# Two half-filled experts in one slot: packing the rests of a mixture-of-experts layer

## The chip, the core and the metric

The kernel runs on one core of a Trainium2 chip. A core has a matrix engine (TensorE, PE in the profile; its weight loads are a row of their own, PEld), a vector engine (VectorE, DVE), a scalar engine (ScalarE, ACT), a general engine (GpSimd, POOL), a queue engine (SyncE, SP) and 16 DMA engines. The metric is the device time of one execution in microseconds (us), the median of several runs.

## The reference

Two layers work on `x` of 3327 rows by 256, with one 0/1 adjacency matrix of 3327 by 3327. Each layer is a graph part and a mixture-of-experts part, both added to `x`. The graph part of layer 0 and its experts, cut to what matters:

```python
x = x + _L0_gnn_ref(_layernorm(x), adj, W, b)     # mean over neighbours, times W
h = _layernorm(x)
probs = softmax(h @ gate_w + gate_b)              # 16 experts
top_probs, top_idx = top_k(probs, 2)              # each row goes to two experts
# for a row of expert e: y = (silu(h @ w1[e]) * (h @ w2[e])) @ w3[e], width 512 inside
x = x + sum over its two experts of  y * (top_prob / sum of both)
```

Layer 1 does the same with an attention-weighted graph part and 6 experts of three 256 by 256 matrices, also top 2 of 6.

## The kernel before

The work is in four stages, one after another with overlaps at the seams: graph of layer 0, slots of layer 0, graph of layer 1, slots of layer 1.

**Graph stages.** The function `graph` goes over column blocks of the transposed adjacency matrix. DVE turns each piece into a mask (L670), PE multiplies (L784), and a chain of small steps (`finish`, `dispatch`) follows each block: normalize, gate products (L810), softmax and top 2 on DVE, and a write of each row's number and weight into the list of its expert in DRAM (L371, indirect DMAs of POOL). Once all rows are routed, `slot_table` computes on DVE, from the counts per expert, which expert and which place in the list each slot has.

**Slots of layer 0.** A slot is 128 rows of one expert. `slots0` is a loop in which the parts of several slots stand side by side. For slot s+1 SP reads the expert's number from the table into a register and loads the hidden weights w1 and w2 (`load0_hidden`), for slot s the output weights w3 (`load0_out`); a load is skipped if the buffer already holds that expert. There are two sets of weight buffers, `w0[s % 2]`, and the table alternates between an expert of the first eight and one of the last eight, so that an expert's slots all use one set. SP also reads the place in the list and fetches 128 entries (`places`, L552); POOL gathers the rows (L560); PE transposes them (L579), makes the two hidden products (L956: 8 products each of 128x128 weights against 128 columns), ACT and DVE form silu times the other (L960, L964), PE makes the output product (L972: 4 products of 128x256), DVE multiplies by the routing weight (L975), and POOL adds the rows into DRAM (`rows_added`, L586). An add waits for the one before it. All three weight loads, the register reads and the list fetches of a slot stand in the one queue of SP, in the order of the loop.

There are 61 such slots (`USUAL0`): the usual number of slots when each expert's rows are rounded up to 128. If the routing needs more, a branch runs up to six more. The first 9 slots (`EARLY0`) have a table of their own and start before the graph stage has ended. The last 8 (from `LATE0`) add into a second tensor, so that the first can be read back before they are done. In the loop also stand loads and masks for the next graph stage (`graph1_ahead`), and one piece per slot of a repacking of the weights of layer 1 (`packs`, on ACT's queue).

**Slots of layer 1** are alike, with 256 rows each (L1137, L1149, L1152, L1154). Near their end four tiles `z` of 1 MB are cleared by DVE (L1187) before the results are read into them.

**Order of the work.** The program states an order, and a scheduler at build time arranges each engine's instructions by estimated times[...]. `tc.issue_after(x)` keeps an instruction behind `x`.

Of the kernel before, what the change touches and what calls it, by code (L numbers as in the profile page):

```python
# [25 lines left out]
def kernel(  # L26
# [52 lines left out]
    SLOTS0 = (2 * N - E0) // P + E0  # L79
# [10 lines left out]
    USUAL0 = min(SLOTS0, int(2 * N / P + E0 / 2 + (E0 / 12) ** 0.5))  # L90
# [8 lines left out]
    assert 2 * EARLY0 < LATE0  # L99

# [73 lines left out]
    later.append(halves_later)  # L174

# [114 lines left out]
    def dispatch(blk, logits, E, rows_of, seen, second_softmax):  # L290
# [78 lines left out]
        for j in range(n):  # L369
            for i in range(2):  # L370
                few_under_way("list", nc.gpsimd.indirect_dma_start(  # L371
                    out=rows_of[2 * (t0 + j) + i],
                    out_offset=bass.IndirectOffsetOnAxis(ap=idx[:, i, j : j + 1], axis=0),
                    in_=where[:, t0 + j, i, :], in_offset=None, bounds_check=E * NP - 1, oob_is_err=False,
                ))

    def slot_table(E, seen, size, slot_p, first=None, taken=None, two=False, low=None, late=None, finals=False):
# [18 lines left out]
        nc.vector.tensor_scalar(nt, ps[:, :E], float(0 if first else size - 1), None, op0=OP.add)  # L396
# [95 lines left out]
        out = small("s_out", 5, I32)  # L492
# [11 lines left out]
        return (out, had) if first else out  # L504

# [48 lines left out]

    def rows_in(who, of):

        n = who.shape[1]
        xg = io.tile([P, n, D], F32, name="xg", bufs=5 if n == 1 else 3)
        for h in range(n):
            last["pool"] = nc.gpsimd.indirect_dma_start(  # L560
                out=xg[:, h, :], out_offset=None, in_=of,
                in_offset=bass.IndirectOffsetOnAxis(ap=who[:, h, 1:2], axis=0),
            )
            if n > 1:
                few_under_way("slot", last["pool"])
        return xg
# [17 lines left out]
    def rows_added(who, y, to):  # L584

        nc.gpsimd.indirect_dma_start(  # L586
            out=to, out_offset=bass.IndirectOffsetOnAxis(ap=who[:, 0, 0:1], axis=0),
            in_=y, in_offset=None, compute_op=OP.add,
        )
# [113 lines left out]
    AHEAD = 3  # L703

    def graph_pools(name, st):
        y = st.enter_context(tc.tile_pool(name=f"y{name}", bufs=1, side="right")).tile([P, NT, 2, D], F32R, name=f"y{name}")
        return y, *(st.enter_context(tc.tile_pool(name=f"{n}{name}", bufs=b, side="right"))
                    for n, b in (("adjs", AHEAD), ("big", AHEAD), ("tmp", 4)))

# [5 lines left out]
    def graph(name, prepare, value, op, wx, update, after, steps, routed, between=None, pools=None, ahead=(), ready=None):  # L715
        adj_ahead, masks_ahead = ahead or ({}, {})
        with ExitStack() as st:
            y, adjs, big, tmp = pools or graph_pools(name, st)
# [198 lines left out]
    early = {}  # L917

# [22 lines left out]

    def load0_hidden(s, which):
        for i, w in enumerate((ffn0_w1, ffn0_w2)):
            load(w0[s % 2][i], lambda e: w[e].rearrange("o (p k) h -> p (o k) h", k=KD), which)

    def load0_out(s, which):
        load(w0[s % 2][2], lambda e: ffn0_w3[e].rearrange("o (a p b) d -> p (o a) b d", p=P, b=2), which)

    def hidden0(s, xT):
        ps = []  # L950
        for w in w0[s % 2][:2]:
            q = bank(2 if s < EARLY0 or s % 2 else 1, [P, NC0, P])
            for c in range(NC0):
                for k in range(KD):
                    h0 = (c // 2) * 2 * P + c % 2
                    nc.tensor.matmul(q[:, c, :], w[:, k, h0 : h0 + 2 * P - 1 : 2], xT[:, k, :],  # L956
                                     start=(k == 0), stop=(k == KD - 1))
            ps.append(q)
        hid = io.tile([P, NC0, P], F32, name="hid", bufs=2)
        silu = nc.scalar.activation(hid, ps[0], AF.Silu)  # L960
        if s >= EARLY0 + 4 and packs:
            with tc.issue_after(silu.ins):
                nc.scalar.dma_start(*packs.pop(0))
        last["silu"], last["hid"] = silu, nc.vector.tensor_mul(hid, hid, ps[1])  # L964
        last["act"], last["dve"] = last["silu"], last["hid"]
        return hid

    def out0(s, who, hid):
        w3 = w0[s % 2][2]
        ps = bank(1 if s < EARLY0 else 0, [P, 512])  # L970
        for c in range(NC0):
            last["slot"] = nc.tensor.matmul(ps[:, :D], hid[:, c, :], w3[:, c // 2, c % 2, :],  # L972
                                            start=(c == 0), stop=(c == NC0 - 1))
        y = io.tile([P, D], F32, name="y", bufs=4)
        nc.vector.tensor_scalar(y, ps[:, :D], weight(who, 0), None, op0=OP.mult)  # L975
        rows_added(who, y, xd_of[0] if s < EARLY0 else xd if s < LATE0 else xe)
# [4 lines left out]
    table0 = slot_table(E0, seen0, P, slot_p, taken=early["had"], two=True, low=seen_head, late=LATE0 - EARLY0)  # L981

    def table0_of(s):
        return (early["table"], s) if s < EARLY0 else (table0, s - EARLY0)
# [3 lines left out]
    def slots0(first, end):  # L988
        for s in range(first - 4, end + 1):
            if not first and s >= 2 * EARLY0 and s % 5 == 0 and s // 5 - AHEAD_AT < 2 * AHEAD:  # L990
                graph1_ahead(s // 5 - AHEAD_AT)
            if not first and s == 2 * EARLY0:
                or_any(table0, early["bad"])
            if not first and s == end - 4:
                early["more"] = asked(*table0_of(end))
            if first <= s + 1 < end:
                which[s + 1] = expert(*table0_of(s + 1), E0)
                load0_hidden(s + 1, which[s + 1])
            if first <= s < end:
                load0_out(s, which.pop(s))  # L1000
            known = EARLY0 if s < EARLY0 - 3 else end
            for i in range(max(who, default=-1) + 1, min(s + 6, known)):
                who[i] = places(*table0_of(i), E0, lists[0], P)
# [9 lines left out]
            if first <= s - 1:  # L1013
                out0(s - 1, who[s - 1], hid.pop(s - 1))
            if not first:
                head1(s - LATE0)
# [3 lines left out]
    pools1 = graph_pools("1", graph1)  # L1020
    ahead1 = {}, {}
# [68 lines left out]
    stage.close()  # L1090

# [9 lines left out]
    def after1(blk, hT):  # L1101
        n = len(blk)
        rh = work.tile([P, BT * P], F32, name="rh")
        ps = ps_mm.tile([P, BT * P], F32, name="mm")
        for k in range(KD):
            nc.tensor.matmul(ps[:, : n * P], small["rw1"][:, k, :], hT[:, k, : n * P], start=(k == 0), stop=(k == KD - 1))  # L1106
        nc.scalar.activation(rh[:, : n * P], ps[:, : n * P], AF.Relu, bias=small["rb1"])
        yield
        logits = choose(n, [rh], [small["rw2"]], E1, small["rb2"])
        yield  # L1110
        yield from dispatch(blk, logits, E1, views[1], seen1, True)
        yield
# [31 lines left out]
    def out1(s, who, h2):  # L1144
# [7 lines left out]
        last["dve"] = nc.vector.tensor_tensor(y, ps, w1s[s % 3][:, None, WB:BB].to_broadcast([P, 2, D]), op=OP.add)  # L1152
# [15 lines left out]
    def slots1(first, end):  # L1168
        for s in range(first - 3, end + 1):
# [15 lines left out]
            if not first and 0 <= s - LATE1 + len(LOW) < len(LOW):  # L1185
                z = zs[s - LATE1 + len(LOW)] = tail.tile([P, BT, 2, D], F32, name="z")
                nc.vector.memset(z, 0.0)  # L1187
# [62 lines left out]
```

## Time and profile before

| | |
|---|---|
| timed runs | 1063.59, 1067.03, 1070.9 us; median 1067.03 |
| the profiled execution | 1096.1 us, of which its span (first to last instruction) 1093.9 us |
| granted PE clock, mean | 0.947 |
| PE busy | 971.7 us |
| graph stage of layer 0, with the early slots at its end | 0 to about 290 us |
| the other slots of layer 0 | about 290 to 600 us |
| graph stage of layer 1 | about 600 to 850 us |
| slots of layer 1 and the end | about 850 to 1094 us |

How to read the lines. On the page a row of an engine gives its busy time, share of the span and number of instructions. A row of a timeline gives start, duration, engine, line of the kernel, operation, output<-inputs, shape and, in brackets, how long the engine had been idle and what ended that. Rows of like instructions are merged (x16). The program's f32 products appear as two instructions each. A row of a stage table gives the stretch in us, its length, the busy time of PE, PEld, DVE, ACT and POOL with the number of instructions, the granted PE clock, the mean share of the DMA engines that was busy, and GB/s.

### The profile page before, as it was taken

Reading aid. Unit: us, or ns where it says so; the run is one execution under the profiler, and the core shown is the slowest. Engines: PE = TensorE matmul, PEld = TensorE weight load, DVE = VectorE, ACT = ScalarE, POOL = GpSimd, SP = SyncE. Lnnn points to the kernel's source line nnn. Section 1 sums busy time; section 2 is a strip of 40 time slices with the busy share of each in tenths; the row PEclk is TensorE's granted clock in tenths of the full one; section 3 lists DMA queues with packets and bytes.
Section 4 is the critical chain, followed back from the end, with each engine's and each line's share of the span. In section 5 each row is a group of like instructions: output and inputs, shape, how many; then the busy total and the mean of one; then the engine's idle time right before and its main releaser. Section 6 shows DMA issues by size and latency. Waiting matters only on the chain. (4 is left out here: it accounts for less than half of the span.)

```text
span 1093.9 us, 17590 instructions
## 1 busy us (share of the span) xinstructions
PE 971.7 (89%) x5404; PEld 838.1 (77%) x5404; DVE 475.9 (44%) x1817; ACT 263.2 (24%) x556; POOL 415.3 (38%) x404
## 2 busy tenths in 40 slices
PE   7999988889899999999999789998986886989871
PEld 5778866779899999999998678876774675877750
DVE  6657565446222222122125386856843461112153
ACT  2312111223111111111114052222222332433320
POOL 2130154155544443443452411014416545556531
PEclk9999999799999999999999889999987898999986
DMA  9986694948858586667678699678491245645695
GB/s 335 339 295 205 232 297 105 319 121 260 252 117 258 124 223 178 169 170 190 166 185 257 152 277 298 181 248 213 121 303 30 74 148 179 240 140 188 203 308 176
DMA packets 122634, 226.33 MB, mean 207 GB/s; under 512 B 32258, under 2 KB 74626, under 8 KB 122540
## 3 DMA queue, kind: packets, MB, share of 16 engines
q1 hardware_dynamic: 76350, 169.29, 47.7%
q0 software_dynamic: 23664, 34.23, 14.6%
q10 hardware_dynamic: 22526, 21.67, 6.3%
q8 instruction: 44, 0.72, 0.3%
q14 instruction: 50, 0.41, 0.1%
HBM read 249.79 MB, written 39.46 MB: 264 GB/s over the span
## 5 line engine op out<-in xcount | busy, mean ns | idle before, releaser
L784 PE MATMUL acc<-big,y 128*128 128x512 f32 (+2 forms) x1456 | 354.3, 398 | 31.3 <-DVE big L670 20.5
L784 PEld LDWEIGHTS acc<-big,y 128*128 128x128 f32 (+1 forms) x1456 | 270.1, 198 | 88.1 <-DVE big L670 10.0
L956 PE MATMUL acc<-xT,w 128*128 128x128 f32 x1952 | 245.1, 284 | 1.6 <-DMA w<-in_ffn_w 1.6
L956 PEld LDWEIGHTS acc<-xT,w 128*128 128x128 f32 x1952 | 238.9, 198 | 2.3 <-PE acc L956 1.0
L371 POOL DMA_INDIRECT list<-where,t_idx x104 | 109.2, 1050 | 179.2 <-DVE t_idx L368 77.4
L560 POOL DMA_INDIRECT xg<-hd,who x119 | 116.6, 980 | 127.8 <-PE acc L579 44.0
L670 DVE TENSOR_SCALAR big<-adj 128x1536 fp32r<-128x1536 int32 (+8 forms) x136 | 112.0, 827 | 108.4 <-DMA adj<-in_adj_t 68.0
L586 POOL DMA_INDIRECT xd<-y,who x53 | 83.6, 1577 | 150.7 <-DMA xd<-y,who 71.9
L964 DVE TENSOR_TENSOR hid<-hid,acc 128x512 f32<-128x512 f32 x61 | 41.9, 688 | 199.1 <-PE acc L956 183.7
L972 PE MATMUL acc<-w,hid 128*128 128x256 f32 x488 | 116.8, 383 | 3.0 <-DVE hid L964 2.7
L972 PEld LDWEIGHTS acc<-w,hid 128*128 128x128 f32 x488 | 88.6, 192 | 13.3 <-DVE hid L964 3.1
L1140 ACT ACTIVATE h<-acc,v 128x256 f32<-128x256 f32 x116 | 54.6, 474 | 123.8 <-PE acc L1137 99.1
L594 POOL DMA_INDIRECT zd<-y,who x58 | 58.5, 1008 | 52.0 <-DVE y L1154 23.5
L581 ACT COPY xT<-mm 128x256 f32<-128x256 f32 (+1 forms) x74 | 32.2, 436 | 188.2 <-PE mm L579 140.9
L1137 PE MATMUL acc<-xT,v 128*128 128x256 f32 x232 | 67.7, 416 | 10.8 <-DMA v<-w1d 4.6
L1137 PE MATMUL acc<-h,v 128*128 128x256 f32 x232 | 64.2, 395 | 11.9 <-ACT h L1140 8.5
L1152 DVE TENSOR_TENSOR y<-acc,v 128x512 f32<-128x512 f32 x29 | 20.1, 692 | 121.0 <-PE acc L1149 69.9
L1137 PEld LDWEIGHTS acc<-xT,v 128*128 128x128 f32 x232 | 46.4, 212 | 22.8 <-issue 6.7
L1137 PEld LDWEIGHTS acc<-h,v 128*128 128x128 f32 x232 | 44.0, 199 | 23.6 <-ACT h L1140 13.2
L1149 PE MATMUL acc<-v,h 128*128 128x256 f32 x232 | 58.9, 392 | 1.3 <-ACT h L1140 0.9
L960 ACT ACTIVATE hid<-acc 128x512 f32<-128x512 f32 x61 | 36.4, 597 | 86.7 <-PE acc L956 79.9
L286 ACT ACTIVATE ln_h<-xs,ln_nmr,ln_rstd 128x256 f32<-128x256 f32 x58 | 30.5, 591 | 92.1 <-DVE ln_nmr L283 57.5
(265 smaller groups left out, 879.2 us busy)
## 6 DMA issues: line engine op xcount, KB each, us to landing
w<-in_ffn_w SPq DMA_DIRECT2D x183, 512.0 KB
adj<-in_adj_t SPq DMA_DIRECT2D x66, 768.0 KB
v<-w1d SPq DMA_DIRECT2D x29, 898.0 KB
adj<-in_adj_t SPq DMA_DIRECT2D x50, 512.0 KB
hd<-ln_h ACTq DMA_DIRECT2D x12, 512.0 KB
z<-zd SPq DMA_DIRECT2D x6, 1024.0 KB
adj<-in_adj_t SPq DMA_DIRECT2D x8, 765.0 KB
w1d<-in_ffn_w ACTq DMA_DIRECT2D x18, 256.0 KB
```

The source lines that it names most:

```text
L371: few_under_way("list", nc.gpsimd.indirect_dma_start(out=rows_of[2 * (t0 + j) + i], out_offset=bass.IndirectOffsetOnAxis(ap=idx[:, i, j : ...
L560: last["pool"] = nc.gpsimd.indirect_dma_start(out=xg[:, h, :], out_offset=None, in_=of, in_offset=bass.IndirectOffsetOnAxis(ap=who[:, h, 1 ...
L586: nc.gpsimd.indirect_dma_start(out=to, out_offset=bass.IndirectOffsetOnAxis(ap=who[:, 0, 0:1], axis=0), in_=y, in_offset=None, compute_op= ...
L594: last["z"] = nc.gpsimd.indirect_dma_start(out=zviews[n * s + h], out_offset=bass.IndirectOffsetOnAxis(ap=who[:, h, 0:1], axis=0), in_=y[: ...
L670: last["mask"] = nc.vector.tensor_scalar(mask[:kr, :, :cols], a[:kr, :, :cols], value, None, op0=op)
L784: last["graph"] = nc.tensor.matmul(acc[c][k][:, :w], y[:kr, j, part, k * P : (k + 1) * P], mask[:kr, jj, i0 : i0 + w], start=(j == 0 and p ...
L956: nc.tensor.matmul(q[:, c, :], w[:, k, h0 : h0 + 2 * P - 1 : 2], xT[:, k, :], start=(k == 0), stop=(k == KD - 1))
L964: last["silu"], last["hid"] = silu, nc.vector.tensor_mul(hid, hid, ps[1])
L972: last["slot"] = nc.tensor.matmul(ps[:, :D], hid[:, c, :], w3[:, c // 2, c % 2, :], start=(c == 0), stop=(c == NC0 - 1))
L1137: ins = nc.tensor.matmul(ps[:, c, :], w[:, k, c : H1 : NC1], src[:, k, :], start=(k == 0), stop=(k == 1))
L1140: last["act"] = nc.scalar.activation(dst[:, c, :], ps[:, c, :], AF.Relu, bias=w1s[s % 3][:, BB + 2 * i + c : BB + 2 * i + c + 1])
L1149: nc.tensor.matmul(ps[:, h, :], h2[:, c, h * P : (h + 1) * P], w[:, c, :], start=(c == 0), stop=(c == NC1 - 1))
```

## The change

Each expert's rows are still cut into slots of 128, but a rest of at most 64 rows no longer takes a whole slot. Two such rests, of two experts, share a slot: rows 0 to 63 are one, 64 to 127 the other. There are 51 full slots (`FULL0`) and 6 pair slots (`PAIRS0`), 57 in all; the pair slots stand at 22, 26, 31, 35, 40 and 44 in the sequence (`PAIR_AT`). Each half has its own weights, in a third and a fourth set of buffers (`wp`, 24 KB per partition), which are loaded without condition during the slots before the pair, one or two 512 KB pieces per slot (`load0_half`). The hidden products of a pair are twice as many with 64 columns each; the output products are twice as many, each giving 64 output rows, the second half's in partitions 64 to 127. A second table (`halves_table`) is computed on DVE from the counts.

```diff
     def hidden0(s, xT):
...
+                for j, (lo, hi) in enumerate(((0, H), (H, P)) if s in PAIR_AT else ((0, P),)):
+                    for k in range(KD):
+                        nc.tensor.matmul(q[:, c, lo:hi], weights0(s)[j][i][:, k, h0 : h0 + 2 * P - 1 : 2], xT[:, k, lo:hi],
+                                         start=(k == 0), stop=(k == KD - 1))
...
     def out0(s, who, hid):
         ps = bank(1 if s < EARLY0 else 0, [P, 512])
         for c in range(NC0):
+            for j, (lo, hi) in enumerate(((0, H), (H, P)) if s in PAIR_AT else ((0, P),)):
+                last["slot"] = nc.tensor.matmul(ps[lo:hi, :D], hid[:, c, lo:hi], weights0(s)[j][2][:, c // 2, c % 2, :],
+                                                start=(c == 0), stop=(c == NC0 - 1))
```

The loads of a half, and the fetch of its places in the list:

```diff
+    def load0_half(p, i, j):
+        with in_order():
+            e = nc.sync.value_load(early["halves"][2 * p + j : 2 * p + j + 1, 0:1], min_val=0, max_val=E0 - 1)
+        last["who"] = nc.sync.dma_start(wp[j][i], (hidden_of if i < 2 else out_of)((ffn0_w1, ffn0_w2, ffn0_w3)[i], bass.ds(e, 1)))
...
+    def half_places(table, h, E, rows_of):
+        who = io.tile([P, 1, 3], I32, name="who", bufs=16)
+        second = io.tile([H, 3], I32, name="second", bufs=8)
+        for i in range(2):
+            with in_order():
+                at = nc.sync.value_load(table[h + i : h + i + 1, 1:2], min_val=0, max_val=E * NP)
+            for t in (who[i * H : (i + 1) * H, 0, :], second)[: i + 1]:
+                last["who"] = nc.sync.dma_start(t, rows_of[bass.ds(at, H), :])
```

In the loop, and the adds, which are two per pair and, for the early slots 2 to 8, stand behind the last list write:

```diff
+            if not first and s == EARLY0 + 3:
+                with tc.issue_after(last["hid"].ins):
+                    early["halves"] = halves_table(E0, seen0, early["had"])
...
+            for p, at in enumerate(PAIR_AT):
+                if first <= at < end:
+                    then = PAIR_AT[p - 1] if p and PAIR_AT[p - 1] >= first else max(first - 1, at - 5)
+                    for n in range(6):
+                        if s == (then + n * (at - 1 - then) // 4 if n < 4 else max(at - 1, then + 1)):
+                            load0_half(p, n // 2, n % 2)
...
+        with tc.issue_after(last["list"].ins) if 2 <= s < EARLY0 else nullcontext():
+            for lo, hi in ((0, H), (H, P)) if s in PAIR_AT else ((0, P),):
+                at = seconds.pop(s)[:, 0:1] if lo else who[:hi, 0, 0:1]
+                nc.gpsimd.indirect_dma_start(
+                    out=to, out_offset=bass.IndirectOffsetOnAxis(ap=at, axis=0),
+                    in_=y[lo:hi, :], in_offset=None, compute_op=OP.add,
+                )
```

Two edits touch layer 1. The space of the pair buffers is handed to the `tmp` pool of its graph stage, which now has five buffers instead of four and also holds `rh`. And the clearing of `z` is kept behind the `y` of its slot:

```diff
-        rh = work.tile([P, BT * P], F32, name="rh")
+        rh = tmps["1"].tile([P, KD, BT * P], F32, name="aT")[:, 0, :]
...
-                nc.vector.memset(z, 0.0)
+                with tc.issue_after(last["y"].ins):
+                    nc.vector.memset(z, 0.0)
```

## The prediction

> **What bounds the kernel now.** I read the page first (engines, slices), then the stage table of the slot section of layer 0, then the timeline of TensorE inside it, then the queue of SP, and last the timeline of DVE and PE near the end of the second graph stage, because the diff also moves a memset there.
>
> ```profile
> PE 971.7 (89%) x5404; PEld 838.1 (77%) x5404; DVE 475.9 (44%) x1817; ACT 263.2 (24%) x556; POOL 415.3 (38%) x404
> ```
> PE is busy 89% of the span. The slots of layer 0 after the nine early ones take about 299 to 598 us. The stage table (columns: stretch, PE, weight loads, DVE, ACT, POOL, PE clock, DMA share, GB/s) has it full:
> ```profile
> 299.00:598.00 299.00, 297.04 (x2179) 286.16 (x2178) 71.46 (x152) 55.97 (x114) 126.05 (x99) 1.00 0.70 188
> ```
> PE idles 2 of 299 us, so a slot costs what PE needs for it; DMA has 0.30 to spare. One slot, and for comparison the gate products, which have only 16 moving columns under the same 128x128 weights (each f32 product is two instructions):
> ```profile
> 119.85 1.85 PE L810 MATMUL mm<-gw,aT 128*128 128x16 f32 x16
> ...
> 322.01 0.39 PE L579 MATMUL mm<-ident,xg 128*128 128x128 f32 x2
> 322.23 3.93 PE L956 MATMUL acc<-xT,w 128*128 128x128 f32 x32
> 326.00 1.89 PE L972 MATMUL acc<-w,hid 128*128 128x256 f32 x8
> 327.73 0.39 PE L579 MATMUL mm<-ident,xg 128*128 128x128 f32 x2
> ```
> From transposes to transposes, 322.01 to 327.73, a slot takes 5.72 us: 0.22 transposes, 3.77 hidden (16 products of 0.236), 1.73 output (4 products of 0.432). The gate row: a lone product lasts 0.29, so 8 of them step at (1.85 - 0.29) / 7 = 0.223 us. **An eighth of the columns is only 6% cheaper[...].**
>
> SP issues the loads. A slot in which nothing is loaded (the repeat skips its weights):
> ```profile
> 449.60 0.79 SPq L545 DMA_DIRECT2D w<-in_ffn_w  x3
> 452.07 0.35 SPq L552 DMA_DIRECT2D who<-list  x1
> 453.98 1.69 SPq L545 DMA_DIRECT2D w<-in_ffn_w  x3
> ```
> SP needs 449.60 to 453.98 = 4.38 us per slot, most of it three register reads of 0.8 to 1 us in the gaps. That is 1.3 less than PE's 5.72.
>
> Last, the end of the second routing:
> ```profile
> 876.19 1.76 DVE L1187 MEMSET z<- 128x2048 f32 x1 [0.38 <-issue]
> 877.87 0.11 DVE L309 TENSOR_TENSOR t_p<-logits,t_m 128x12 f32<-128x12 f32 x1
> 877.89 0.60 DVE L1154 TENSOR_SCALAR y<-y,who 128x256 f32<-128x256 f32 x2
> 878.87 1.76 DVE L1187 MEMSET z<- 128x2048 f32 x1 [0.37 <-issue]
> 880.85 0.17 DVE L311 TENSOR_REDUCE t_s<-t_p 128x2 f32<-128x12 f32 x1 [0.22 <-issue]
> ```
> ```profile
> 912.25 1.14 PE L579 MATMUL mm<-ident,xg 128*128 128x128 f32 x4 [5.72 <-DMA xg<-hd,who]
> 915.84 0.70 PE L579 MATMUL mm<-ident,xg 128*128 128x128 f32 x2 [2.45 <-DMA xg<-hd,who]
> ```
> Four memsets of 1.76 us lie between the steps of the dispatch whose table, list and gather PE then waits 8 us for.
>
> [...]
>
> **Does it do what it says?** I worked the routing from the reference's inputs: the 16 experts get 324 to 511 rows. Rounded up to 128 they fill exactly 61 slots. With rests of at most 64 split off they give 51 full slots and 10 halves, so 6 pair slots with two halves empty: 57, and the conditional extra slots stay skipped as before. The built order of PE agrees: a pair slot has 32 hidden products of 64 columns and 8 output products of 64x256; full slots are unchanged.
>
> **The change, part by part.**
> 1. Ten slots go (61 = 51 + 10): -10 x 5.72 = -57.2 us.
> 2. Six pair slots come. Transposes 0.22. Hidden: 32 products instead of 16, since each half has its own weights. I take 0.223 (gate row; its 16 columns and the 128 of L956 bracket 64): 7.14; at 0.236 it is 7.55. Output: 8 products, each still streaming 256 columns, 0.432. In series 3.46; wholly side by side 1.73[...]. A pair: 0.22 + 7.14 + 2.18 = 9.54, times 6 = 57.2. **So on PE the trade is even: 0.0 us**, with bounds 6 x 9.09 - 57.2 = -2.7 and 6 x 11.23 - 57.2 = +10.2.[...]
> 3. Weights. Pair buffers are loaded without condition: 12 experts x 1.57 MB = 18.9 MB, all issued during slots 17 to 43. At 332 GB/s for a share of 0.94 (first 25 us) that is 53 us of all engines. These 27 slots before: 27 x 5.72 = 154 us at share 0.70 = 108. After: 22 full + 5 pairs = 22 x 5.72 + 5 x 9.54 = 174 us, of which 161 busy: share 0.93. SP: a pair period (3.4 full slots and one pair, 29 us of PE) costs 4.4 x 4.38 = 19.3, plus six reads and issues of 1.5 = 9, plus 1.7 for the second half's places, minus 3 for the pair's own skipped expert reads: 27 us of 29. A full expert's w1 and w2 can start only when the buffer's last slot is done, and have one slot, about 7.7 us. Eight such loads fall in this stretch; each finds at most one or two halves (1.6 us each) ahead of it. I take 0.5 us for each: +4; bounds 0 (before, PE's waits for weights were 1.9 us in all) and 8 x 2.5 = 20.
> 4. The table of the halves: some 75 small DVE operations, 60 of them between two hid products. Before, 41 such operations between two hids took 270.71 to 276.54, 0.14 each; 60 need 8.5 us against a slot of 5.72. PE has one hidden phase in hand, so 0 to 4; I take +1.
> 5. Adds. They go one after another, 4.45 us apart at best, 7 at worst (386.60 to 393.79). Six more, of half size, in a stretch of pairs that PE itself needs 9.5 us for; four y buffers cover: +1, bounds 0 and 6. Early adds 2 to 4 move behind the last four list writes; the order of POOL puts the same adds and lists ahead of the first gather as before: 0, bounds -4 and +2.
> 6. Memsets leave the dispatch for the late slots, behind y, where DVE is busy 5 of 25 us: of 7.06 us the three that sit between its steps give back 5; bounds -7 and 0. What is late next is the list landing, which moves with the same chain. The second stage's rh moves into a pool of five instead of four: 0, its old owners are done by then; at worst 2.
>
> Sum: 0 + 4 + 1 + 1 - 5 = **+1 us**. The profiled execution was 1096.1 us with a span of 1093.9 (2.2 around it), so I expect 1097 there. The timed runs lie lower, median 1067.03; the same difference gives 1068[...].
>
> **Rivals.**
> - *Column halves in series.* Pair 10.82: 6 x 1.28 = +7.7 over my value, 1077. For it: no row of before shows column halves[...].[...]
> - *Slower: SP's queue becomes the bound.* If half loads delay the full experts' loads, each of the 8 waits 2 to 3 us: +20, with the add chain at 7 us per slot behind it; total +17 to +25, 1087. It decides once SP needs more than PE's 29 us per pair period, or DMA more than a share of 1; I have 27 and 0.93. Against: before, the share was 0.83 in whole windows with hardly a wait.
> - *Faster: cost follows columns.* If 64 columns cost 0.118, a pair is 0.22 + 3.77 + 2.18 = 6.17: -20 us, 1048. Against it stands the gate row.
> - *It doesn't fit*: the extra branch runs three pair slots more; the counts speak against it.
>
> **Numbers.** Forecast case 0.53; series 0.19; queue 0.17; faster 0.08; other 0.03. The range 1059 to 1087 takes the forecast with its memset and overlap bounds (-8) and reaches to the middle of the queue case. About 1% (10.7 us) is what a measurement can tell. Slower by more: the queue case 0.17, half of the series case 0.10, tails 0.06: 0.33. Faster by more: 0.08 and 0.03 of tails: 0.11. Within: 0.56.
>
> **What would show it.** Right: a pair slot of 9 to 10 us; 64-column products at 0.22; output halves starting nearly together; slot section as long as before within 8 us; DMA share over 0.85 in it; weight waits of PE under 8 us; PE's wait for the gather near 912 shrunk by about 5. Wrong: 64-column products at half price, or a slot section longer by over 15 us with PE waiting for w or p.

## The result: 3.1% slower

The changed kernel took 1100.8 us (median of 4; 1098.5 to 1104.0), the kernel before on the same chip 1069.0: a ratio of 1.031 (95% interval 1.025 to 1.036). 1069 was forecast, with a range of 1059 to 1087; 1068 comes from the steps, and the last microsecond was the author's estimate, which no trace shows. The profiled execution of the changed kernel took 1102.2 us, its span 1100.3. Executions far above the fastest of the same kernel on the same chip are set aside here, and each ratio compares the others.

One point before the traces are compared: chips differ. The kernel before took 1066 to 1069 us on some and 1103 to 1109 us on others, and its first profile (1096.1 us) fits the latter. Times are therefore set only against the kernel before on the same chip, as ratios, and stages only where the text says from which chip.

The page of the changed kernel: engines, granted clock by slices, and the two groups of hidden products (busy us, mean ns of one, then the idle time before them).
```profile
PE 974.2 (89%) x5478; PEld 843.8 (77%) x5478; DVE 478.4 (43%) x1886; ACT 259.0 (24%) x548; POOL 419.5 (38%) x402
PEclk9999998899899999889979998999999998999986
...
L1070 PE MATMUL acc<-xT,w 128*128 128x128 f32 x1632 | 212.9, 291 | 9.4 <-DMA w<-in_ffn_w 8.8
...
L1070 PE MATMUL acc<-xT,p 128*128 128x64 f32 x384 | 54.8, 310 | 3.1 <-ACT xT L672 3.1
```
PE is busy for only 2.5 us more than in the first profile, stretches at a lower clock included. The clock dips in the slices of the slot section; the loss is idle time and clock. Two stage tables show it (PE, weight loads, DVE, ACT, POOL, PE clock, DMA share, GB/s): first the slot section of the changed kernel, then that of a kernel that has the slots of before (the run "sides" below).
```profile
294.00:641.00 347.00, 324.37 (x2261) 304.03 (x2259) 74.97 (x222) 52.20 (x107) 125.38 (x98) 0.94 0.73 208
```
```profile
294.00:600.00 306.00, 299.98 (x2188) 288.41 (x2187) 75.08 (x169) 59.74 (x122) 129.10 (x100) 1.00 0.69 183
```
The section has grown from 306 to 347 us. In it PE is idle for 347 - 324.4 = 22.6 us instead of 6.0, and the granted clock is 0.94 instead of 1.00, which over 347 us is worth another 21 us, nearly all of it while PE works. The DMA share rose by only 0.04, to 0.73 (0.76 from 340 to 560 us, where the pairs stand): on average the DMA engines are not full.

The first pair, on PE (p are the weights of the pairs' halves):
```profile
379.71 3.41 PE L1070 MATMUL acc<-xT,p 128*128 128x64 f32 x28
382.95 1.95 PE L1086 MATMUL acc<-w,hid 128*128 128x256 f32 x8
384.74 0.39 PE L670 MATMUL mm<-ident,xg 128*128 128x128 f32 x2
385.06 1.95 PE L1086 MATMUL acc<-p,hid 128*64 128x256 f32 x16
386.93 0.50 PE L670 MATMUL mm<-ident,xg 128*128 128x128 f32 x2
```
The pair's 16 output instructions (eight products, four for each column half) take 386.93 - 385.06 = 1.87 us. In series they would take 8 x 0.432 = 3.46. **Column halves run side by side**, and somewhat better than in the forecast, whose 2.18 us was the author's estimate between 1.73 and 3.46: no trace of before shows such products. The 28 hidden instructions of 64 columns take 382.95 - 379.71 = 3.24 us, 0.231 for a product of two: **hardly cheaper than 0.236 for 128 columns.** A pair is 0.22 + 32 x 0.231 + 1.87 = 9.5 us; 9.54 was forecast.

What ends PE's waits in the slot section, after and before (us in total, times, longest). A load of p, one of 36 of 512 KB, is called a half load from here on:
```profile
PE acc L1070 <- DMA w<-in_ffn_w: 8.8, 4, 4.5
PE mm L670 <- DMA xg<-hd,who: 6.4, 3, 3.8
...
PE acc L1086 <- DMA w<-in_ffn_w: 2.1, 1, 2.1
PE acc L1086 <- DMA p<-in_ffn_w: 0.9, 1, 0.9
```
```profile
PE acc L956 <- DMA w<-in_ffn_w: 1.6, 2, 0.9
PE acc L972 <- DMA w<-in_ffn_w: 0.3, 1, 0.3
```
Before, PE waited 1.9 us in all. One wait of the changed kernel, and what follows it:
```profile
430.62 1.89 PE L1086 MATMUL acc<-w,hid 128*128 128x256 f32 x8
436.31 0.70 PE L670 MATMUL mm<-ident,xg 128*128 128x128 f32 x2 [3.80 <-DMA xg<-hd,who]
437.52 7.94 PE L1070 MATMUL acc<-xT,p 128*128 128x64 f32 x36 [0.52 <-ACT xT L672]
445.26 5.63 PE L1070 MATMUL acc<-xT,w 128*128 128x128 f32 x32
...
470.21 6.70 PE L1070 MATMUL acc<-xT,w 128*128 128x128 f32 x32 [4.48 <-DMA w<-in_ffn_w]
```
PE stands 3.80 us for a gather. The 36 instructions that follow take 7.94 us; the same 36 take 4.46 us at 369.64, in the first pair. The clock in four-microsecond stretches:
```profile
436.00:440.00 4.00, 3.18 (x14) 2.79 (x14) 0.00 (x0) 0.37 (x1) 0.97 (x1) 0.50 0.81 256
440.00:444.00 4.00, 4.00 (x21) 4.00 (x20) 0.00 (x0) 0.00 (x0) 2.56 (x2) 0.50 0.30 35
444.00:448.00 4.00, 4.00 (x20) 4.00 (x20) 0.00 (x0) 0.00 (x0) 0.00 (x0) 0.50 0.11 33
448.00:452.00 4.00, 4.00 (x27) 3.87 (x27) 0.69 (x1) 0.60 (x1) 0.00 (x0) 0.89 0.22 66
```
For 12 us after the stall PE runs at half speed, three times as long as the stall itself; with the wait, this place cost about 10 us. The gap of 4.48 us is followed by slow products as well: 6.70 us at 470.21 for what takes 3.93, with a clock of 0.50 from 470 to 474 us. So is a shorter gap, with a clock of 0.57 from 510 to 514 us:
```profile
508.97 5.54 PE L1070 MATMUL acc<-xT,w 128*128 128x128 f32 x32 [2.29 <-DMA w<-in_ffn_w]
```
Here the duration of the half clock does not go with the length of the gap. In this slot section it is longest twice, both times mostly over the 64-column products of a pair: the 12 us above, and from 558 to 572 us, at 0.51, after a gap of only 1.80 us:
```profile
557.24 0.51 PE L670 MATMUL mm<-ident,xg 128*128 128x128 f32 x2 [1.80 <-DMA xg<-hd,who]
557.58 9.88 PE L1070 MATMUL acc<-xT,p 128*128 128x64 f32 x48
```
These 48 instructions take 9.88 us; in another profile of the changed kernel (after_again, below) 48 take 5.76 where PE had not waited for a DMA before them. That profile has the same two places (7.94 us for 36 at 436.03, 9.64 for 48 at 554.62). In the run "bytes", which has no pairs and where PE waits up to 4.5 us for w, the 32 hidden instructions of a slot take 6.39 us at most. So in these traces a stall ahead of a pair cost more than one elsewhere; no run takes the narrow products away at a stall. The forecast had no term for the clock.

Why was the gather late? POOL's queue just before:
```profile
424.10 1.45 POOL L680 DMA_INDIRECT xd<-y,who  x1 [3.53 <-DMA xd<-y,who]
...
429.64 1.41 POOL L680 DMA_INDIRECT xd<-y,second  x1 [4.10 <-DMA p<-in_ffn_w]
...
431.36 1.00 POOL L651 DMA_INDIRECT xg<-hd,who  x1 [0.30 <-issue]
```
The pair's second addition waits 4.10 us. It is the one that must follow the first (the view names a half load as the last event before it; for the same instruction 30 us earlier it names the first addition). In the trace the first addition lands at 428.91 and the second starts 0.73 us later, as the two additions before start 0.77 us after the landing that they wait for. The two gathers behind it on POOL start only at 431.36.

And the stall goes on through SP:
```profile
436.02 0.47 SPq L643 DMA_DIRECT2D second<-list  x1
...
449.02 0.60 ACT L1074 ACTIVATE hid<-acc 128x512 f32<-128x512 f32 x1 [11.55 <-PE acc L1070]
449.03 0.52 ACTq L1077 DMA_DIRECT2D w1d<-in_ffn_w  x1
...
452.18 1.58 SPq L1060 DMA_DIRECT2D p<-in_ffn_w  x2
...
461.04 1.56 SPq L1060 DMA_DIRECT2D p<-in_ffn_w  x2
...
464.47 1.43 SPq L625 DMA_DIRECT2D w<-in_ffn_w  x3
```
SP issues nothing for 16 us. Its next half load waits for the landing of a w1d load that ScalarE issues at 449.03, behind an activation that had itself waited 11.55 us for PE. In the trace the two transfers share a completion semaphore (number 101), and that is the half load's only wait; the products with the weights that it overwrites, among the 36 above, end by 445.46. The wait view of SP counts two such waits (us in total, times, longest):
```profile
SPq L1060 <- DMA w1d<-in_ffn_w: 19.6, 2, 14.9
```
So PE's stall delays an activation, this a transfer on ScalarE's queue, and this SP's next loads. **A stall may breed the next one:** at 470.21 PE waits 4.48 us for w. This last link is argued, not shown. SP issues that w at 464.47, 0.6 us after PE has freed its buffer, so SP's delay does not hold it up directly; it lands 5.6 us later, behind half loads that SP issues late and close together (452.18 to 462.6). All of this is read from one place of the trace, and no run takes the link away alone.

Last, layer 1. The memsets went where the diff puts them, between the late slots; the wait for the gather did not shrink: 8.90 us, where 5.72 + 2.45 were seen before.
```profile
1005.24 1.76 DVE L1322 MEMSET z<- 128x2048 f32 x1 [0.38 <-issue]
```
```profile
929.73 1.38 PE L670 MATMUL mm<-ident,xg 128*128 128x128 f32 x4 [8.90 <-DMA xg<-hd,who]
```

### The profile page after: what moved, and what is told of

The parts are those of the page before. It is cut to its first block, busy times and chain, and to the rows that moved or that the text cites. A ratio compares the mean times of both kernels' runs of the same rounds, so it can differ in the third digit from the quotient of the medians.

```text
span 1100.3 us, 17772 instructions
## 1 busy us (share of the span) xinstructions
PE 974.2 (89%) x5478; PEld 843.8 (77%) x5478; DVE 478.4 (43%) x1886; ACT 259.0 (24%) x548; POOL 419.5 (38%) x402
## 5 line engine op out<-in xcount | busy, mean ns | idle before, releaser
L882 PE MATMUL acc<-big,y 128*128 128x512 f32 (+2 forms) x1456 | 346.1, 391 | 33.8 <-DVE big L764 20.4
L882 PEld LDWEIGHTS acc<-big,y 128*128 128x128 f32 (+1 forms) x1456 | 263.6, 193 | 88.6 <-ACT y L1180 10.2
L1070 PE MATMUL acc<-xT,w 128*128 128x128 f32 x1632 | 212.9, 291 | 9.4 <-DMA w<-in_ffn_w 8.8
L1070 PEld LDWEIGHTS acc<-xT,w 128*128 128x128 f32 x1632 | 207.5, 205 | 10.6 <-issue 7.1
L680 POOL DMA_INDIRECT xd<-y,who x49 | 76.8, 1568 | 173.2 <-DMA xd<-y,who 60.4
L1086 PE MATMUL acc<-w,hid 128*128 128x256 f32 x408 | 101.3, 393 | 4.8 <-DVE hid L1078 2.7
L1086 PEld LDWEIGHTS acc<-w,hid 128*128 128x128 f32 x408 | 76.0, 196 | 14.1 <-DVE hid L1078 5.3
L670 PE MATMUL mm<-ident,xg 128*128 128x128 f32 x184 | 37.0, 300 | 27.9 <-DMA xg<-hd,who 27.9
L670 PEld LDWEIGHTS mm<-ident,xg 128*128 128x128 f32 x184 | 32.7, 201 | 36.8 <-DMA xg<-hd,who 30.8
L1070 PE MATMUL acc<-xT,p 128*128 128x64 f32 x384 | 54.8, 310 | 3.1 <-ACT xT L672 3.1
```

Source lines behind the costliest of these rows:

```text
L670: nc.tensor.transpose(ps[:, k, h * P : (h + 1) * P], xg[:, h, k:D:KD], ident)
L680: nc.gpsimd.indirect_dma_start(out=to, out_offset=bass.IndirectOffsetOnAxis(ap=at, axis=0), in_=y[lo:hi, :], in_offset=None, compute_op=OP ...
L882: last["graph"] = nc.tensor.matmul(acc[c][k][:, :w], y[:kr, j, part, k * P : (k + 1) * P], mask[:kr, jj, i0 : i0 + w], start=(j == 0 and p ...
L1070: nc.tensor.matmul(q[:, c, lo:hi], weights0(s)[j][i][:, k, h0 : h0 + 2 * P - 1 : 2], xT[:, k, lo:hi], start=(k == 0), stop=(k == KD - 1))
L1086: last["slot"] = nc.tensor.matmul(ps[lo:hi, :D], hid[:, c, lo:hi], weights0(s)[j][2][:, c // 2, c % 2, :], start=(c == 0), stop=(c == NC0 ...
```

## Experiments

Six sets, each on one chip (A is that of the result). "Slots" is the time from the first late slot, whose transposes wait for a gather, to the first product of the second graph stage, read from PE's timeline of the one profiled execution of each run.

| chip, before (us) | run | ratio (95%) | slots, us |
|---|---|---|---|
| A, 1069.0 | changed kernel | 1.031 (1.025 to 1.036) | 360.9 |
| B, 1102.6 | base_again | | 313.2 |
| | noloads | 1.004 (1.001 to 1.007) | 324.3 |
| | thin | 1.007 (1.003 to 1.010) | 323.9 |
| | late | 1.023 (1.016 to 1.031) | 347.6 |
| C, 1065.8 | after_again | 1.036 (1.028 to 1.045) | 360.6 |
| | half | 1.014 (1.004 to 1.024) | 331.7 |
| | act | 1.035 (1.025 to 1.045) | 358.4 |
| | sides | 1.006 (1.003 to 1.009) | 317.3 |
| D, 1108.4 | memset | 0.998 (0.995 to 1.001) | 313.2 |
| | adds | 1.002 (0.999 to 1.006) | |
| | oneadd | 1.020 (1.012 to 1.029) | 341.2 |
| | whole | 1.000 (0.998 to 1.003) | 310.9 |
| E, 1109.2 | after3 | 1.026, of two executions, no interval | 356.8 |
| | oneadd2 | 1.023 (1.017 to 1.029) | 344.4 |
| | noloads2 | 1.002 (0.999 to 1.005) | |
| | neither | 1.005 (1.001 to 1.008) | 326.1 |
| F, 1067.9 | bytes | 1.019 (1.011 to 1.026) | 344.4 |
| | latefirst | 1.017 (1.010 to 1.025) | 335.1 |

The slot section hardly depends on the chip (313 to 317 us with the slots of before; 357 to 361 in three profiles of the changed kernel); the other stages do.

**base_again**: no edit.

> The kernel before, once more, for its profile: the first profiled execution of it took 1096.1 us, its timed runs 1063.6 to 1071.6. Expected: a profiled execution of 1064 to 1075 us, in which the slot section of layer 0 lasts about 315 us as it did in the first profile, and the rest about 25 us less than there. If the profiled execution is again near 1096 us, profiles of before are slower than its timed runs for a reason of their own, and stages of before and after can't be set against each other directly.

1101.3 us on a chip where the kernel before had a median of 1102.6; slots 313.2, against 314.6 in the first profile. The first profile was thus not odd in its stages; most likely it came from such a chip, which the record does not name.

**noloads**: the half loads of all but the first pair are left out, register reads and transfers.
```diff
-                        if s == (then + n * (at - 1 - then) // 4 if n < 4 else max(at - 1, then + 1)):
+                        if (p == 0 or first) and s == (then + n * (at - 1 - then) // 4 if n < 4 else max(at - 1, then + 1)):
                             load0_half(p, n // 2, n % 2)
```


> The changed kernel without the half loads of the pairs after the first: neither their register reads nor their transfers; these pairs use the first pair's weights again, so their output is of the wrong experts. The changed kernel took 1100.8 us, the one before 1069. Loads theory (SP's queue held up by them, or their bytes): 1068 to 1075, the loss is all in the loads. Theory of the pair's two additions in series on GpSimd, which hold up the gathers: 1092 to 1100. Theory that pair slots cost more on PE: 1092 to 1100.

1.004: **nearly the whole loss goes with the loads**, and with the pairs but without their loads the kernel is within 1% of the one before. Their slot section is 11 us longer than before (six waits of 0.52 us on the copy of xT, 3.3 us of waits for weights near the first pair, which still loads), and part of that is given back later. A stall of 2.49 us here, for w at 363, is not followed by a half clock: it stays at 1.00.
```profile
362.00:366.00 4.00, 1.51 (x12) 1.32 (x12) 0.69 (x1) 0.00 (x0) 1.58 (x1) 1.00 0.94 314
366.00:370.00 4.00, 4.00 (x30) 3.83 (x29) 0.48 (x1) 0.60 (x2) 1.74 (x2) 1.00 0.66 159
```

**thin**: same reads, places and waits, thin transfers.
```diff
+        if 0 < p < PAIRS0:
+            to, of = (to[:, 0, :32], of[:, 0, :32]) if i < 2 else (to[:, 0, 0, :32], of[:, 0, 0, :32])
         last["who"] = nc.sync.dma_start(to, of)
```


> The changed kernel with all half loads issued at the same places of SP's queue and with the same waits, but only 32 of the elements of each partition loaded for the pairs after the first (wrong weights for these). Head-of-line theory (SP stands at a half load whose buffer the last pair still reads, and the full experts' loads and lists stand behind it): within 8 us of the changed kernel, 1092 to 1100. Bytes theory (15.7 MB more through the same DMA engines): 1068 to 1078. If half and half: 1080 to 1088.

1.007, slots as in noloads. **SP's instructions and its waits for the pair buffers cost about 0.3%, within the noise, when the transfers are small; the bytes are needed for the loss.** PE's waits for weights in the section:
```profile
PE acc L1089 <- DMA w<-in_ffn_w: 2.1, 1, 2.1
...
PE acc L1073 <- DMA w<-in_ffn_w: 0.2, 1, 0.2
```

**late**: the first four half loads of each later pair were to be issued later, where their buffer is free. The formula issues 11 of these 20 loads one slot later, 7 in the same slot and 2 a slot earlier, so the run tests less than its expectation says.
```diff
-    if s == (then + n * (at - 1 - then) // 4 if n < 4 else max(at - 1, then + 1)):
+    if s == (then + n * (at - 1 - then) // 4 if n < 4 and (not p or first) else
+             min(then + 1 + n // 2, at - 1) if n < 4 else max(at - 1, then + 1)):
```


> The changed kernel with the first four half loads of each later pair issued one or two slots later, where the buffers are free or nearly free when SP comes to them; same bytes. Head-of-line theory: 1076 to 1088, most of the loss comes back. Bytes theory: 1098 to 1106, no gain, since the same bytes have less time. GpSimd or PE theory: 1099 to 1103, no change.

1.023, slots some 10 us shorter than in the changed kernel. By the slot section the place of the half loads in SP's queue does cost something with full bytes, about a third of the loss, less than the head-of-line theory had. Its reason, the pair's buffers, is not what the wait view names (w1d loads), so the run shows a size and not the reason; and as the intervals of 1.023 and of the changed kernel overlap, and the chips differ, the size is rough.

**after_again**: no edit.

> The changed kernel once more, beside the others on one chip: in the first set of experiments the chip ran the kernel before in 1102.6 us, not in 1069, so only ratios carry over. Expected: 1.031 times the kernel before (1.025 to 1.036), and a slot section of layer 0 that is 40 to 48 us longer than the 313 us of the kernel before on that chip.

1.036; slots 43.3 us longer than those of sides on this chip; the timed runs are 33.5 us longer than those of sides and 39.8 longer than those of the kernel before. The loss is in the slot section.

**half**: one of two slices of every half load after the first pair.
```diff
+        if 0 < p < PAIRS0:
+            to, of = to[:, 0], of[:, 0]
```


> The changed kernel with the half loads of the pairs after the first cut to half their bytes (one of two slices of each tile), at the same places of the queue. Without these loads the ratio to the kernel before was 1.004, with thin ones 1.007, with all bytes 1.031. If the cost goes with the bytes: 1.018 to 1.020. If only a load that is long enough to push a full expert's load past its slot costs anything: under 1.011. If the number of large transfers counts: 1.025 or more.

1.014, between the cases. In the slot section half the bytes cost 331.7 - 324.3 = 7 us over none (another chip), the other half 29 us. But the profiled execution is the fastest of the four (1072.7 us, median 1077.1). By the ratios the first half costs 0.010 and the second 0.022, and with the interval of half (1.004 to 1.024) a cost in proportion to the bytes, 1.020, is not ruled out. **That the cost grows faster than the bytes is likely, and not shown.**

**act**: ScalarE reads and issues the half loads after the first pair.
```diff
+        by = nc.scalar if 0 < p < PAIRS0 else nc.sync
+            e = by.value_load(early["halves"][2 * p + j : 2 * p + j + 1, 0:1], min_val=0, max_val=E0 - 1)
+        ins = by.dma_start(wp[j][i], ...)
```


> The changed kernel with the half loads of the pairs after the first read and issued by ScalarE instead of SyncE, so that they travel in ScalarE's queue and not ahead of the full experts' loads in SyncE's. Same bytes. Order theory (the full experts' loads wait behind half loads in the one queue): 1.008 to 1.018. Bandwidth theory (the same engines carry the same bytes, so the full loads are slowed all the same): 1.025 to 1.035. Worse than 1.035 if ScalarE's copies and activations are held up by the register reads and the waits for the pair's buffers.

1.035: no gain from another queue. That speaks for the engines' capacity and against the order within SP's queue, but not cleanly: PE now waits 5.3 us for p itself, and ScalarE's copies of xT stand 15.7 us behind half loads.

**sides, memset, adds**: the kernel before with the change's side edits, both and each alone.
```diff
-                nc.vector.memset(z, 0.0)
+                with tc.issue_after(last["y"].ins):
+                    nc.vector.memset(z, 0.0)
```
```diff
+        with tc.issue_after(last["list"].ins) if 2 <= s < EARLY0 else nullcontext():
+            nc.gpsimd.indirect_dma_start(
```


> The kernel before with two side edits of the change alone, no pair slots: the memsets of the last four z tiles are issued behind the late layer-1 slots, and the early additions 2 to 4 behind the last list write. The prediction gave the memsets -5 us (-7 to 0) and the additions 0 (-4 to +2): ratio 0.995 (0.990 to 1.002). In the run without half loads layer 1 took 239 us against 245.5 before, which agrees with -5. If that gain came from the pairs' different end of layer 0 and not from the memsets: 0.999 to 1.001.

> The kernel before with the memset edit alone (the last four z tiles are set behind the late layer-1 slots). With the additions' order as well the ratio to the kernel before was 1.006 (1.003 to 1.009), where the prediction had 0.995. If the memsets gain their 5 us and the additions lose 10: 0.995 (0.991 to 0.999). If the memsets lose (they now sit among the outputs of the late slots on VectorE): 1.004 to 1.008, and the additions do nothing.

> The kernel before with the order of the early additions alone (2 to 4 behind the last list write). If the additions lose 10 us and the memsets gain 5: 1.008 to 1.012. If the memsets are what loses: 0.998 to 1.002.

Both on chip C: 1.006. Alone on chip D: memsets 0.998, additions 1.002. None of the expectations fits all three; the parts on D do not sum to C's 1.006, and it stays open whether the chip makes the difference. The memset edit may be worth up to 5 us there (interval -5.5 to +0.9); its gain is not shown.

**oneadd, and oneadd2 beside the changed kernel on chip E**: the pairs' second addition is left out, and with it 64 rows of each pair in the sum.
```diff
-            for lo, hi in ((0, H), (H, P)) if s in PAIR_AT else ((0, P),):
+            for lo, hi in ((0, H),) if s in PAIR_AT else ((0, P),):
```


> The changed kernel without the second of the two additions of each pair (its second 64 rows are left out of the sum). The changed kernel is at 1.036 (1.028 to 1.045) of the kernel before on the last chip, with 8 us of waits for gathers on PE and a half clock after them. GpSimd theory (the second addition waits 4 to 5 us for the first and holds up the gathers queued behind it): 1.018 to 1.026. Bytes theory: 1.031 to 1.037.

> The changed kernel, one corner of four beside the next three runs on one chip. 1.025 to 1.040 of the kernel before.

> The changed kernel without the pairs' second additions, now on the same chip as the changed kernel. If the additions hold up gathers: 0.010 to 0.018 below the changed kernel's ratio, no wait of PE for a gather in the slot section, and a slot section some 15 to 20 us shorter. If the bytes alone count: within 0.004 of it.

> The changed kernel without the half loads after the first pair, on this chip: 1.001 to 1.008 of the kernel before, the ratio of the first set.

> The changed kernel without the half loads after the first pair and without the second additions. If the two causes simply add: as far below the run without half loads as the run without second additions is below the changed kernel (0.010 to 0.018). If the additions only cost something because gathers are late already, through the loads: within 0.004 of the run without half loads.

With the loads, the slot section is 12 us shorter without the second additions on chip E (344.4 against 356.8), and 12 to 20 us over all profiles. The timed runs are less sure. Against the changed kernel on A and C the ratio falls by 0.008 to 0.016; on E, where only two executions of after3 count, it falls from 1.026 to 1.023, which tells nothing. Without the loads the second additions cost nothing (ratios 1.005 without them, 1.002 with; sections 326.1 without, 324.3 with, on another chip). By the sections, then, **the two causes need each other**; by the timed runs this is not settled.

The expected end of the gather waits came. The only wait of PE for a gather in oneadd and oneadd2 is the one with which the section starts in every kernel (6.1 and 5.5 us), where after_again has 8.3 us after it. How the additions cost their 12 us on chip E is another matter: after3 has only 1.1 us of gather waits inside the section, and from 300 to 600 us its idle time is that of oneadd2 (21.2 and 20.6 us). What differs is the clock, 0.93 against 0.97 there: in after3 it is 0.86 from 400 to 450 us and 0.90 from 500 to 600, in oneadd2 0.93 or more in every 50 us, and there none of the pairs' 64-column products is slow (36 take 4.45 us, 48 take 5.76).

**whole**: noloads, and the pairs after the first computed as full slots (all rows by one expert's weights, half the products).
```diff
-                for j, (lo, hi) in enumerate(((0, H), (H, P)) if s in PAIR_AT else ((0, P),)):
+                for j, (lo, hi) in enumerate(((0, H), (H, P)) if s in PAIR_AT[:1] + PAIR_AT[PAIRS0:] else ((0, P),)):
```


> The run without half loads (ratio 1.004), with the pairs after the first also computed as full slots: all 128 rows by the first half's weights, 16 hidden products and 4 output products instead of 32 and 8. A pair slot took 9.7 us on PE and a full one 5.72: if PE bounds the pairs, 5 x 3.98 = 20 us less, and 2 us of waits on the copy of xT go with it: 0.982 to 0.986. If the pairs are bound by their two additions or by SyncE's queue: above 0.995.

1.000. Some 20 us of PE's work went. The slot section is 13 us shorter than that of noloads (another chip) and the ratio 0.004 lower; against the slots of before on the same chip (memset, 313.2) the section is only 2 us shorter. PE now waits elsewhere:
```profile
PE mm L670 <- DMA xg<-hd,who: 11.7, 7, 5.5
PE acc L882 <- ACT y L1180: 10.9, 1, 10.9
```
Six waits for gathers inside the section, 6.2 us in all (the seventh, 5.5 us, is the one with which the section starts); these gathers stand on POOL behind additions that follow one another. And a longer wait just after the section, which the kernels before and without loads also have (6.9 and 8.8 us). **Behind PE the next bound stood at almost the same length.** So even with free loads and pairs as cheap as full slots, this change did not gain (0.998 to 1.003).

**bytes**: the 61 slots of before, with the 36 half loads added at their places in SP's queue, into buffers that nothing reads (experts fixed, no register reads). To make room for the buffers, the graph stage's temporary pool opens later, as in the change.
```diff
+    LOAD_AT = [22, 26, 31, 35, 40, 44]
...
+                for p, at in enumerate(LOAD_AT):
+                    then = LOAD_AT[p - 1] if p else at - 5
...
+                            to, e = wp[n % 2][n // 2], 2 * p + n % 2
...
+                                last["who"] = nc.sync.dma_start(to, ffn0_w3[e : e + 1].rearrange("o (a p b) d -> p (o a) b d", p=P, b=2)
...
```


> The kernel before, its 61 slots untouched, with the 36 half loads of 512 KB added at the places where the changed kernel has them in SyncE's queue. They go to buffers that nothing reads, of experts fixed beforehand, so without register reads and without waits for a pair. If the bytes are the cause: 1.012 to 1.025, and PE waits for w and xg in the slot section, followed by a half clock. If the loads only hurt together with the pairs (waits for pair buffers, their two additions): 0.999 to 1.006.

1.019, 20 us (12 to 28), as the bytes case had it: **the bytes alone, with no pair in the kernel, cost about half of the loss.** The size is that of this kernel: the 36 loads fall here into a stretch of 61 equal slots, which is shorter than that of the pairs. PE's waits in the slot section, one of them with SP's queue before it, and the stage table around it:
```profile
PE acc L961 <- DMA w<-in_ffn_w: 13.3, 5, 4.5
PE mm L579 <- DMA xg<-hd,who: 6.4, 5, 2.5
```
```profile
422.91 0.96 SPq L545 DMA_DIRECT2D w<-in_ffn_w  x3
...
425.26 2.58 SPq L1028 DMA_DIRECT2D p<-in_ffn_w  x2
...
429.39 1.46 SPq L545 DMA_DIRECT2D w<-in_ffn_w  x3
...
432.17 1.35 SPq L1028 DMA_DIRECT2D p<-in_ffn_w  x2
...
436.17 4.18 PE L961 MATMUL acc<-xT,w 128*128 128x128 f32 x18 [4.39 <-DMA w<-in_ffn_w]
```
```profile
428.00:432.00 4.00, 3.79 (x26) 3.39 (x24) 1.09 (x2) 0.70 (x2) 2.55 (x2) 1.00 0.90 307
432.00:436.00 4.00, 0.00 (x0) 0.00 (x0) 0.08 (x1) 0.25 (x1) 0.00 (x0) 0.75 1.03 335
436.00:440.00 4.00, 3.83 (x18) 3.86 (x19) 0.00 (x0) 0.04 (x1) 2.56 (x2) 0.50 1.02 410
440.00:444.00 4.00, 4.00 (x26) 3.80 (x26) 0.69 (x1) 0.56 (x1) 0.00 (x0) 0.90 1.08 364
```
From 428 to 444 us the engines are full: shares of 0.90 to 1.08, 307 to 410 GB/s. The w that PE needs at 436 is issued among two pairs of p; it lands in this burst, PE stands 4.39 us, and the clock is 0.50 in the next stretch. From 340 to 560 us as a whole the share is 0.83, and says nothing of this. Nor is a burst alone enough: in the first profile of the kernel before the share is 1.02 from 340 to 350 us, and PE is busy throughout. What hurt at 436 us is a burst around a load that PE needed next.

**latefirst**: late, and each gather ahead of the pair's additions on POOL.
```diff
-        with tc.issue_after(last["list"].ins) if 2 <= s < EARLY0 else nullcontext():
+        with tc.issue_after(last["list"].ins) if 2 <= s < EARLY0 else tc.issue_after(last["pool"].ins) if s in PAIR_AT[:PAIRS0] else nullcontext():
```


> The changed kernel mended at two places: the half loads issued later, as in the run of the first set (1.023 there), and each gather put ahead of the pair's additions in GpSimd's queue. Same bytes. If waits in queues are what the two hold: 1.008 to 1.018. If the bytes set a floor that no order passes: 1.018 to 1.026. Below the kernel before only if both waits were the whole loss: under 1.004.

1.017: about half of the loss goes with the two queue orders mended, and what stays is what the bytes cost alone (1.019 on the same chip). PE waits for no gather inside the section, and less for weights:
```profile
PE acc L1070 <- DMA w<-in_ffn_w: 5.7, 2, 4.0
```
Of the forms of the change that leave nothing out it has the lowest ratio in these runs, and it is still slower than before.

## Why the prediction was wrong

- **Step 1** (-57.2): right. A full slot still takes 5.73 us (300.23 to 305.96 on PE).
- **Step 2** (pairs +57.2, PE even): right, 9.5 us a pair. Left out was the wait on xT, 0.52 us a pair, 3 us in all. The rival "column halves in series" falls with the 1.87 us, the rival "cost follows columns" with the 0.231.
- **Step 3** (weights, +4): **the step that failed.** The bytes alone measured +20 us (bytes), and with the pairs' queue orders the loss is 33 to 39. Three things were wrong in it. It took a DMA share forecast at 0.93 on average as room; from 340 to 560 us the share came out at 0.76, and the engines were still full in the bursts that decide (1.01 from 466 to 470 us, where PE waits for w). It gave each of eight loads 0.5 us; four waits for w were 8.8 us together. And it priced a stall at its own length, where stalls of 1.8 to 4.5 us were followed by a clock of 0.50 to 0.57, worth 21 us over the section. The upper bound of +20 covered the bytes alone, and had nothing for the clock, which stayed low longest, 12 and 14 us, mostly over the pairs' own products.
- **Step 4** (table, +1): right; the hidden phases around it, 300 to 350 us, keep PE busy throughout in noloads.
- **Step 5** (additions +1, bounds 0 to 6): too small. Alone they cost next to nothing, as forecast; together with late loads 12 to 20 us of the section, in single profiles. They were costed by themselves, and the "four y buffers" that were named as its cover do not cover the gathers behind it. The early additions (0, bounds -4 to +2): +2.7 us measured, -1.7 to 6.9; not told apart from nothing.
- **Step 6** (memsets, -5): not shown; -2.3 us alone, -5.5 to +0.9, and the wait for the gather, which was to shrink by 5, did not shrink in the changed kernel.
- The **rival "SP's queue becomes the bound"** had the right place and sign, and at 1087 it was nearest. Its price was too low and its point of decision wrong: neither SP, which stands waiting for over 60 of the 220 us from 340 to 560, nor the mean DMA share passed the limits named, and thin shows that SP's time costs almost nothing.

The sum that the runs support: pairs without their loads +2 to +4 us; pairs with all bytes in the better queue orders +19, no more than the bytes cost alone; in the orders of the change +33 to +39, so that some 14 to 20 us go with the orders. These are differences between chips, and the two executions on chip E (1.026) would make it +29.

Open: how the second additions cost their part, through gathers or through the clock; how far act's result comes from shared engines and how far from ScalarE's own waits; the side edits' 1.006 on one chip; and what a third weight buffer for the full experts would do, which was not tried.

## What to carry over

Price added transfers in the stretch between a buffer coming free and its next use, not by the mean share of the stage: in bytes that was 0.83, and 0.90 to 1.08 where PE stood. Price a stall of PE twice: its length, and the half clock that may follow it. Here stalls of 1.8 to 4.5 us were followed by a clock of 0.50 to 0.57 for 4 to 14 us, longest where narrow products came next, and one of 2.49 us by none. And before buying back work of the busiest engine, ask how far behind the second one is: taking the work away in one run shows it (whole: 20 us of PE's work, a ratio of 1.000).

## What was not expected of the hardware

Eight output products of 64 rows and 256 columns in two column halves took 1.87 us, 8% more than four whole ones (1.73). A clock of 0.50 held for 12 us after one stall of 3.80 us, and one of 0.51 for 14 us after one of 1.80, in both cases mostly over 64-column products. And the same kernel took 1066 and 1068 us on two chips and 1103 to 1109 on three others: with nearly the same slot section (317.3 and 313.2 us with the slots of before), but 235 to 241 us on the former two chips (C, F) against 254 to 267 on the latter three (B, D, E) from the last adjacency product of the second graph stage to the end.
